# Attention in a fused hybrid network: test, mask load, division and norm in other places, and image 3's scores masked by VectorE

## The chip, the cores and the metric

The kernel runs on one NeuronCore of one Trainium2 chip. The metric is the time on the device in microseconds (us). The engines of a core run side by side, each through its own queue in order: PE (TensorE, matrix products, with PEld for its weight loads), DVE (VectorE), ACT (ScalarE), POOL (GpSimd) and SP (SyncE, which issues DMAs here).

## What is computed

The reference is a chain of six layers over four images of 32 x 32 positions and 256 channels (L = 1024 tokens per image). Layer 0 is a selective scan (Mamba-like) with 512 inner channels and 64 states; then come a grouped convolution, the attention with which this change deals, a mixture of 8 experts, a second selective scan with 16 states, and a second mixture. The attention, per image, with 8 heads of 32 channels:

```python
Q, K, V = (proj(Wq, bq), proj(Wk, bk), proj(Wv, bv))
scores = jnp.einsum('bhnd,bhmd->bhnm', Q, K) / jnp.sqrt(jnp.float32(hd))
mask = jnp.zeros((N, N), dtype=bool).at[edge_index[0], edge_index[1]].set(True)
scores = jnp.where(mask[None, None], scores, -jnp.inf)
attn = jax.nn.softmax(scores, axis=-1)
attended = jnp.einsum('bhnm,bhmd->bhnd', attn, V)
out = attended @ Wo + bo
y = x + out            # then a layer norm, times gamma, plus beta
```

The two scans are recurrences over the tokens, h = dA * h + (dt * x) * B and y = sum over states of h * C.

## The kernel before, in words

**Scans.** A scan is cut into units of 128 partitions (channels times states) by 1024 tokens, 1280 units in all. For a unit, SP loads dt broadcast into a tile dA, ACT takes its exp, PE spreads the input over the states into PSUM (`ps_rep`, two banks, tag x, two buffers), DVE multiplies `ps_rep` by B in place and runs the recurrence (`tensor_tensor_scan`), POOL multiplies by C, and after every second unit PE sums over the states (`ps_y`). `scans` (L351) writes this order: at step k it looks for chunks of input to load (`chunks_ahead`, L397), loads unit k+4, spreads unit k+1 (`first`), takes the exp of unit k+2 and scans unit k. The scans' order is `SCANS` (L31): layer 0 of image 0 and 1, layer 3 of image 0, and so on; layer 3 of image 3 is the last, and its input is made by image 3's stage "middle".

**Stages.** All else is written as Python generators in a list `STAGES` (L33): front (layer 0's projections), middle (`back0`, `layer1`, `attention`, `moe(2)`, `front3`) and last (`back3`, `moe(3)`), each for four images. `run` (L535) weaves them between the scans' instructions: after every half step of the scans it advances the current stage up to two yields, as long as a clock of planned costs per engine (`Metered`, whose `run` is the line L124 that nearly every instruction has) does not run ahead of DVE's. So the order on every engine's queue is fixed at build time. When a chunk's input has not been made within 5 units of its use (`LATEST`), `need` (L500) advances the stage until it has, with no scan units between. That happens once after the start: at unit 1211, five units before the last scan, image 3's stage "middle" is then run from inside attention through the mixture and into `front3`.

**PSUM.** The scans have five banks: `ps_rep` twice two banks, `ps_y` one. The stages have three, two of tag s and one of tag acc; `ps` (L173) hands these out in turn.

**Attention** (L1096). After a norm and a transpose, q, k and v are projected. `shift` (L1167) then tests whether scores can be large: it squares q and k on ACT, sums the squares by head with 64 matmuls of 4 columns (`ps_n2`), reduces on DVE, transposes, and makes a flag `large`. Each of PE, DVE, ACT and SP reads the flag and takes a branch (`tc.Switch`); the branch that finds row maxima is only for large scores and is not taken here, so `mT` stays at its memset's zero. Then the mask of 0 and -1e30 (bf16, 2 MB) is loaded by one DMA (L1149), and for each half nh of the queries and each pair of heads hp, `heads` (L1279) goes through 8 blocks of 128 keys: scores of two heads (`ps_sc`, the tag s, one bank each), plus `mT`, plus the mask through an identity matmul; exp on ACT into `p`; then the values and, through a matrix of ones, the sums, four matmuls side by side in 32 columns each (`ps_at`, tag acc). `pipe` (L179) sets values of block k-1 ahead of scores of block k. After two pairs DVE takes the reciprocal of the sums and POOL multiplies; after four, `attended` (L1325) projects by Wo (`ps_wo`), adds, norms (`lny`) and adds into tb.

Of the kernel before, what the change touches and what calls it, by code (L numbers as in the profile page):

```python
# [7 lines left out]
F32 = mybir.dt.float32  # L8
BF16 = mybir.dt.bfloat16
I32 = mybir.dt.int32  # L10
# [6 lines left out]
P = 128  # L17
# [115 lines left out]
class Hybrid:  # L133
# [217 lines left out]
    def scans(self, mp, psum):  # L351
# [16 lines left out]
        state = {}  # L368
        y = None
# [165 lines left out]
    def run(self):  # L535

        self.done, self.ready = set(), set()
        self.todo, self.stage, self.wait = list(STAGES), None, None
        nc, tc = self.nc, self.tc
# [532 lines left out]
    def prepare2(self, st, psum):  # L1072
# [5 lines left out]
        for k in range(2):  # L1078
# [8 lines left out]
        self.byhead = self.const.tile([P, 4], F32, name="byhead")  # L1087
        nc.vector.tensor_reduce(
            self.byhead, self.ident.rearrange("p (h d) -> p h d", d=HD), AX.X, ALU.add
        )  # L1090
        self.onesb = self.const.tile([P, P], BF16, name="onesb")
# [4 lines left out]
    def attention(self, b, tb):  # L1096
        nc, tc, vec = self.nc, self.tc, self.vec
        with tc.tile_pool(name=f"at{b}", bufs=1, side="right") as op:
# [4 lines left out]
            mT = op.tile([P, 2, L], BF16, name="mT")  # L1103
            wo = self.weight(op, "L2_attn_Wo", 2)
            with tc.tile_pool(name=f"aa{b}", bufs=1, side="right") as fp:
# [24 lines left out]

                def values(j):
# [13 lines left out]
            with tc.tile_pool(name=f"ab{b}", bufs=1, side="right") as fp:  # L1145
                yield from self.shift(fp, qT, kT, mT)
            with tc.tile_pool(name=f"ac{b}", bufs=1, side="right") as fp:
                maskT = fp.tile([P, TB, L], BF16, name="maskT")
                nc.sync.dma_start(maskT, self.mem[("maskT",)].rearrange("j p f -> p j f"))  # L1149
                yield 1.0  # L1150
                for nh in range(2):
                    raw, sums = (
                        fp.tile([P, 2, 512], F32, tag=t, name=t) for t in ("raw", "sums")
                    )
                    for hp in range(4):
                        yield from self.heads(fp, raw, sums, qT, kT, v, maskT, mT, nh, hp)
                        if hp % 2:
                            c = hp // 2
                            nc.vector.reciprocal(sums[:, c, :], sums[:, c, :])
                            yield 2.0  # L1160
                            nc.gpsimd.tensor_tensor(
                                raw[:, c, :], raw[:, c, :], sums[:, c, :], ALU.mult
                            )
                            yield 0.5
                    yield from self.attended(fp, tb, nh, raw, xa, wo)

    def shift(self, fp, qT, kT, mT):  # L1167
# [3 lines left out]
        nc, tc = self.nc, self.tc  # L1171
        nc.vector.memset(mT, 0.0)
        n2 = self.ps("ps_n2", (P, 2, TB * HEADS))
        for i, x in enumerate((qT, kT)):
            sq = fp.tile([P, 2, L], F32, tag="sq", name="sq")
            for c in range(2):
                nc.scalar.activation(sq[:, c, :], x[:, c, :], AF.Square)
                yield 0.5
                for m in range(TB):
                    at = 4 * (2 * m + c)  # L1180
                    nc.tensor.matmul(
                        n2[:, i, at : at + 4], lhsT=sq[:, c, m * P : (m + 1) * P], rhs=self.byhead,
                        start=True, stop=True,
                    )
                yield 1.5
        top = fp.tile([P, 2], F32, name="top2")
        nc.vector.tensor_reduce(top, n2, AX.X, ALU.max)
        yield 0.5
        ps = self.ps("ps_n3", (P, 2, P))
        for i in range(2):  # L1190
            nc.tensor.transpose(ps[:1, i, :], top[:, i : i + 1], self.ident)
        yield 0.5
# [6 lines left out]
        large = fp.tile([1, 1], I32, name="large")  # L1199
        nc.vector.tensor_copy(large, most[:, 0:1])  # L1200
        yield 1.0
        yield 1.0
# [6 lines left out]
        for arm in tc.Switch(go, 2):  # L1209
            if arm == 1:  # L1210
                for _ in self.row_max(fp, qT, kT, mT):
                    pass
# [3 lines left out]
    def row_max(self, fp, qT, kT, mT):  # L1216
# [3 lines left out]
        mask = fp.tile([P, TB, L], BF16, name="mask")  # L1220
        nc.sync.dma_start(mask, self.mem[("maskT",)].rearrange("j p f -> p j f"))
# [57 lines left out]
    def heads(self, fp, raw, sums, qT, kT, v, maskT, mT, nh, hp):  # L1279

        nc = self.nc
        qs = slice(nh * 512, (nh + 1) * 512)
        c, at = hp // 2, 64 * (hp % 2)
        acc = self.psum.tile([P, 512], F32, tag="acc", name="ps_at", bufs=1)
        got = {}

        def scores(kb):
            two = [self.psum.tile([P, 512], F32, tag="s", name="ps_sc", bufs=2) for _ in range(2)]  # L1290
# [6 lines left out]
            for i in range(2):  # L1297
                nc.tensor.matmul(
                    two[i], lhsT=self.onesb[rows[i], :], rhs=mT[rows[i], c, qs],
                    start=False, stop=False,  # L1300
                )
            for i in range(2):
# [3 lines left out]
            got[kb] = p = fp.tile([P, 2, 512], F32, tag="p", name="p", bufs=3)  # L1306
            for i in range(2):
                nc.scalar.activation(p[:, i, :], two[i], AF.Exp)

# [11 lines left out]
        yield from self.pipe(range(TB), scores, values, cost=1.3, cut=True)  # L1321
# [3 lines left out]
    def attended(self, fp, tb, nh, att, xa, wo):  # L1325
# [19 lines left out]
        yield from self.pipe(range(2), project, add, cost=1.7)  # L1345
        yield from self.norm(fp, y, 4, y, "lny")
# [443 lines left out]
```

## Time and profile before

| what | us |
|---|---|
| median of 3 runs (6886.66 to 6919.45) | 6898.74 |
| the profiled execution | 6903.87 |
| its span | 6902.1 |
| mT's memsets in the four attentions, at | 1474.0, 2609.0, 4064.1, 5520.6 |
| last scan before the stretch without scans, at | 5645.6 |
| last head's reciprocal of image 3, at | 5851.2 |

| group (128 partitions) | mean ns of one | count |
|---|---|---|
| DVE scan 1024 | 2285 | 1280 |
| DVE product with `ps_rep` 1024 | 1213 | 1280 |
| POOL product 1024 | 2371 | 1280 |
| ACT exp of scores 512 | 595 | 512 |
| DVE reciprocal 512 | 3353 | 16 |
| PE mask product `ps_sc` 512 | 397 | 512 |

A row of a profile's timeline has the start in us, the duration, the engine, the line, the operation, what it writes and reads, its size and how many rows are merged (xN); in brackets stands the idle time of the engine before it and what ended that. A row of the windows view has the stretch, its length, then the busy time of PE, PEld, DVE, ACT and POOL with their instructions, the granted clock of PE (1.00 is full), the share of the DMA engines and GB/s. Records of PE with f32 operands come twice per matmul.

### The profile page before, as it was taken

What the parts mean: (1) busy time and instruction counts of PE and PEld (TensorE: products, weight loads), DVE (VectorE), ACT (ScalarE), POOL (GpSimd) and SP (SyncE); (2) the same over time, 40 slices, a digit from 0 to 9 for tenths busy, and PEclk for the clock granted to TensorE, in tenths of its full rate; (3) what the DMA queues carried; (4) which work ended last, traced back from release to release, by engine and by line L of the source; (5) the groups of instructions that cost most, each with busy time, mean ns of one, the idle gap of its engine ahead of it and who ended that gap; (6) DMA issues with size and microseconds to landing.
All of it is one profiled execution on the core that took longest, in us unless ns stands there. A gap on an engine that the chain in (4) does not pass through costs nothing. (4 is left out here: it accounts for less than half of the span.)

```text
span 6902.1 us, 66302 instructions
## 1 busy us (share of the span) xinstructions
PE 5422.5 (79%) x20516; PEld 2221.7 (32%) x20516; DVE 5209.3 (75%) x4477; ACT 3437.1 (50%) x4143; POOL 3649.9 (53%) x1801
## 2 busy tenths in 40 slices
PE   6558768678798577879689768798798777867979
PEld 2002213232242032234145322252253322523556
DVE  7778988977898986889889867898899841247411
ACT  2426557344477343557568334477485432244411
POOL 0876776755557754555856545557666620044200
PEclk8558768679799577989789778898698789877989
DMA  1556665754455755446756654456667530145321
GB/s 71 149 143 162 175 176 154 188 136 111 113 164 158 195 145 132 116 127 177 185 151 163 173 136 119 122 144 177 179 165 185 149 86 6 44 122 155 86 61 34
DMA packets 394239, 937.47 MB, mean 136 GB/s; under 512 B 83220, under 2 KB 165729, under 8 KB 392225
## 3 DMA queue, kind: packets, MB, share of 16 engines
q1 hardware_dynamic: 391696, 930.53, 50.5%
q8 instruction: 173, 2.83, 0.2%
q0 software_dynamic: 2128, 2.13, 0.2%
q14 instruction: 242, 1.97, 0.1%
HBM read 842.59 MB, written 93.95 MB: 136 GB/s over the span
## 5 line engine op out<-in xcount | busy, mean ns | idle before, releaser
L124 POOL TENSOR_TENSOR h<-h,rows 128x1024 f32<-128x1024 f32 x1280 | 3030.9, 2371 | 1992.5 <-DVE h L124 1624.7
L124 DVE TENSOR_TENSOR_SCAN h<-dA,ps_rep 128x1024 f32<-128x1024 f32 x1280 | 2924.3, 2285 | 208.3 <-issue 91.3
L124 DVE TENSOR_TENSOR ps_rep<-ps_rep,rows 128x1024 f32<-128x1024 f32 x1280 | 1552.8, 1213 | 344.8 <-PE ps_rep L124 323.6
L124 ACT ACTIVATE dA<-dA,A_L_conv_A_log 128x1024 f32<-128x1024 f32 x1024 | 1152.4, 1145 | 712.4 <-DMA dA<-dt 623.2
L124 PE MATMUL ps_rep<-S,spread_L_conv_A_log 96*128 96x512 bf16 x2048 | 761.7, 463 | 739.7 <-DVE h L124 691.4
L124 PE MATMUL ps_y<-h,collect_L_conv_A_log 128*32 128x512 f32 x4096 | 780.4, 752 | 106.6 <-POOL h L124 105.6
L124 PE MATMUL ps_h<-xTm,we 128*128 128x512 f32 x1536 | 718.1, 607 | 4.3 <-ACT h_m L124 3.2
L124 PE MATMUL ps_e<-we,h_m 128*128 128x256 f32 x3072 | 702.1, 381 | 8.7 <-ACT h_m L124 8.7
L124 ACT ACT_TABLE_LOAD x486 | 623.5, 1283 | 73.8 <-PE ps_h L124 51.0
L124 PEld LDWEIGHTS <-spread_L_conv_A_log 96*128 96x128 bf16 x2048 | 163.6, 104 | 1502.1 <-DVE h L124 1167.0
L124 PEld LDWEIGHTS ps_e<-we,h_m 128*128 128x128 f32 x3072 | 580.5, 190 | 158.9 <-issue 54.0
L124 ACT ACTIVATE p<-ps_sc 128x512 f32<-128x512 f32 x512 | 277.9, 595 | 600.0 <-PE ps_sc L124 599.7
L124 DVE SCALAR_TENSOR_TENSOR tb<-ps_e,cw,tb 128x256 f32<-128x256 f32 x512 | 220.6, 474 | 407.4 <-PE ps_e L124 407.4
L124 ACT ACTIVATE h_m<-ps_h,cols 128x512 f32<-128x512 f32 x384 | 260.7, 687 | 487.5 <-PE ps_h L124 484.6
L124 ACT ACTIVATE dA<-dA,A_L_attn_A_log 128x1024 f32<-128x1024 f32 x256 | 293.5, 1148 | 407.8 <-DMA dA<-dt 376.2
L124 PE MATMUL ps_at<-p,v 128*32 128x512 f32 x1024 | 366.8, 631 | 64.2 <-ACT p L124 56.2
L124 PEld LDWEIGHTS ps_h<-xTm,we 128*128 128x128 f32 x1536 | 291.8, 193 | 339.7 <-issue 289.7
L124 PE MATMUL ps_rep<-S,spread_L_attn_A_log 96*128 96x512 bf16 x512 | 191.3, 464 | 225.4 <-DVE h L124 183.3
L124 PE MATMUL ps_sc<-qT,kT 32*128 32x512 f32 x1024 | 305.0, 671 | 0.0
L124 PE MATMUL ps_at<-p,ones 128*32 128x512 f32 x1024 | 282.2, 631 | 0.0
L124 PEld LDWEIGHTS ps_y<-h,collect_L_conv_A_log 128*32 128x32 f32 x4096 | 102.0, 119 | 493.1 <-POOL h L124 254.1
L124 PE MATMUL ps_cv<-pad,diag 128*128 128x512 f32 x576 | 260.4, 593 | 0.0
(304 smaller groups left out, 5030.5 us busy)
## 6 DMA issues: line engine op xcount, KB each, us to landing
dA<-dt SPq DMA_DIRECT2D x2048, 256.0 KB
dA<-dt SPq DMA_DIRECT2D x2048, 64.0 KB
we<-in_L_ffn_W_dram SPq DMA_DIRECT2D x64, 512.0 KB
parts<-parts SPq DMA_DIRECT2D x64, 384.0 KB
S<-parts SPq DMA_DIRECT2D x96, 256.0 KB
dt<-sp_r SPq DMA_DIRECT2D x64, 256.0 KB
y<-yo SPq DMA_DIRECT2D x128, 128.0 KB
y_back<-y SPq DMA_DIRECT2D x64, 256.0 KB
```

The costliest lines, as they stand in the source:

```text
L124: return got(*args, **kw)
```

## The change

1. The test leaves `shift` and becomes `large_scores`, called after the projections of q and k and ahead of the values. Its sums take 8 matmuls of 512 columns, four side by side, with a `byhead` repeated 8 times; the branch stays where it was.
2. `maskT` moves to attention's outer pool, and its load is issued right after the test.
3. Division, projection and norm of the first half are woven into later heads: after the third yield of a head, each yield is followed by one of a waiting generator `then`. A division goes into the head behind it, the projection of half 0 after the first head of half 1, and its norm into the second.
4. In `scans`, when a chunk's input is late, the next unit's `first` is put off, the unit is finished, and only then is `need` called, with a flag `alone`.
5. Heads that begin with `alone` set make the mask 0 or 1 once, keep their scores in the scans' PSUM (two banks as one tile, two buffers), take one exp over 1024 columns, and mask on DVE: min with 3e38, times the mask. Their pipe has three steps: scores, mask, values. Other heads are as before.

```diff
-        def chunks_ahead(k):
-
-            if k + AHEAD < len(units) and units[k + AHEAD][2:] == (0, 0, 0):
+        def chunks_ahead(k, late=False):
+            if not late and k + AHEAD < len(units) and units[k + AHEAD][2:] == (0, 0, 0):
                 waiting.append(k + AHEAD)
             while waiting:
                 scan, d = units[waiting[0]][:2]
-                if waiting[0] - k > LATEST and ("parts", *scan, d) not in self.ready:
-                    break
+                if ("parts", *scan, d) not in self.ready:
+                    if waiting[0] - k > LATEST:
+                        break
+                    if not late:
+                        return True
+                    self.alone = True
                 chunk(waiting.pop(0))
+                self.alone = False
+            return False
...
-            chunks_ahead(k)
+            waits = chunks_ahead(k)
             load(k + 4)
-            first(k + 1)
+            if not waits:
+                first(k + 1)
...
+            if waits:
+                chunks_ahead(k, True)
+                first(k + 1)
             yield
...
+    def all_heads(self, fp, tb, qT, kT, v, maskT, mT, xa, wo):
+        nc = self.nc
+        def divided(raw, sums, c):
+            nc.vector.reciprocal(sums[:, c, :], sums[:, c, :])
+            yield 2.0
+            nc.gpsimd.tensor_tensor(raw[:, c, :], raw[:, c, :], sums[:, c, :], ALU.mult)
+            yield 0.5
+        then = iter(())
+        self.zero_one = False
+        for nh in range(2):
+            raw, sums = (fp.tile([P, 2, 512], F32, tag=t, name=t, bufs=2) for t in ("raw", "sums"))
+            for hp in range(4):
+                for n, cost in enumerate(self.heads(fp, raw, sums, qT, kT, v, maskT, mT, nh, hp)):
+                    yield cost
+                    if n >= 3:
+                        more = next(then, None)
+                        if more is not None:
+                            yield more
+                yield from then
+                then = iter(())
+                if nh and hp == 0:
+                    y = yield from self.projected(fp, 0, first, xa, wo)
+                    then = self.normed(fp, tb, 0, y)
+                if hp % 2:
+                    then = divided(raw, sums, hp // 2)
+            first = raw
+        yield from then
+        y = yield from self.projected(fp, 1, raw, xa, wo)
+        yield from self.normed(fp, tb, 1, y)
...
+    def large_scores(self, fp, qT, kT, large):
...
+        for i, x in enumerate((qT, kT)):
             for c in range(2):
+                nc.scalar.activation(sq[:, i, c, :], x[:, c, :], AF.Square)
+                yield 0.8
+        for g in range(2):
+            n2 = self.ps("ps_n2")
+            for r in range(4):
+                nc.tensor.matmul(
+                    n2[32 * r : 32 * r + 32, :], lhsT=self.byhead.rearrange("p h k -> p (h k)"),
+                    rhs=sq[:, r // 2, r % 2, g * 512 : (g + 1) * 512],
+                    start=True, stop=True, tile_position=(0, 32 * r),
+                )
+            nc.vector.tensor_reduce(top[:, g : g + 1], n2, AX.X, ALU.max)
+            yield 1.3
...
+        alone = self.alone
+        if alone and not self.zero_one:
+            self.zero_one = True
+            for kb in range(TB):
+                nc.vector.tensor_scalar(maskT[:, kb, :], maskT[:, kb, :], -1.0, None, ALU.is_ge)
...
         def scores(kb):
-            two = [self.psum.tile([P, 512], F32, tag="s", name="ps_sc", bufs=2) for _ in range(2)]
+            if alone:
+                both = self.scan_psum.tile([P, 2, 512], F32, tag="x", name="ps_sx", bufs=2)
+                two = [both[:, i, :] for i in range(2)]
+            else:
+                two = [self.psum.tile([P, 512], F32, tag="s", name="ps_sc", bufs=2) for _ in range(2)]
...
+            if alone:
+                nc.scalar.activation(p, both, AF.Exp)
+                return
...
+        def masked(kb):
+            nc.vector.scalar_tensor_tensor(
+                got[kb], got[kb], 3.0e38, maskT[:, kb, qs].unsqueeze(1).to_broadcast([P, 2, 512]),
+                ALU.min, ALU.mult,
+            )
...
-        yield from self.pipe(range(TB), scores, values, cost=1.3, cut=True)
+        if alone:
+            yield from self.pipe(range(TB), scores, masked, values, cost=1.3)
+        else:
+            yield from self.pipe(range(TB), scores, values, cost=1.3, cut=True)
```

More of the change, by code (lines that the diff above doesn't have):

```diff
@@ L368, in scans @@
         state = {}
+        self.scan_psum = psum
         y = None
@@ L538, in run @@
         self.todo, self.stage, self.wait = list(STAGES), None, None
+        self.alone = False
         nc, tc = self.nc, self.tc
@@ L1086, in prepare2 @@
         nc.vector.tensor_scalar(self.bq, vec["L2_attn_bq"], self.isq, None, ALU.mult)
-        self.byhead = self.const.tile([P, 4], F32, name="byhead")
+        byhead = st.tile([P, 4], F32, name="byhead4")
         nc.vector.tensor_reduce(
-            self.byhead, self.ident.rearrange("p (h d) -> p h d", d=HD), AX.X, ALU.add
+            byhead, self.ident.rearrange("p (h d) -> p h d", d=HD), AX.X, ALU.add
         )
+        self.byhead = self.const.tile([P, 4, 8], F32, name="byhead")
+        nc.vector.tensor_copy(self.byhead, byhead.unsqueeze(2).to_broadcast([P, 4, 8]))
         self.onesb = self.const.tile([P, P], BF16, name="onesb")
@@ L1103, in attention @@
             mT = op.tile([P, 2, L], BF16, name="mT")
+            maskT = op.tile([P, TB, L], BF16, name="maskT")
             wo = self.weight(op, "L2_attn_Wo", 2)
+            large = op.tile([1, 1], I32, name="large")
+            nc.vector.memset(mT, 0.0)
             with tc.tile_pool(name=f"aa{b}", bufs=1, side="right") as fp:
@@ L1129, in attention @@
                 )
+                yield from self.large_scores(fp, qT, kT, large)
+                nc.sync.dma_start(maskT, self.mem[("maskT",)].rearrange("j p f -> p j f"))
                 def values(j):
@@ L1145, in attention @@
             with tc.tile_pool(name=f"ab{b}", bufs=1, side="right") as fp:
-                yield from self.shift(fp, qT, kT, mT)
+                yield from self.shift(fp, qT, kT, mT, maskT, large)
             with tc.tile_pool(name=f"ac{b}", bufs=1, side="right") as fp:
[L1148 to L1173, printed above, removed]
+                yield from self.all_heads(fp, tb, qT, kT, v, maskT, mT, xa, wo)
+    def all_heads(self, fp, tb, qT, kT, v, maskT, mT, xa, wo):
[27 more added lines that the diff above has]
+        yield from self.normed(fp, tb, 1, y)
@@ L1174, in shift @@
+    def large_scores(self, fp, qT, kT, large):
+        nc = self.nc
+        sq = fp.tile([P, 2, 2, L], F32, name="sq")
+        top = fp.tile([P, 2], F32, name="top2")
         for i, x in enumerate((qT, kT)):
-            sq = fp.tile([P, 2, L], F32, tag="sq", name="sq")
             for c in range(2):
[L1177 to L1192, printed above, removed]
+                nc.scalar.activation(sq[:, i, c, :], x[:, c, :], AF.Square)
[10 more added lines that the diff above has]
+            yield 1.3
@@ L1193, in shift @@
+        nc.vector.tensor_tensor(top[:, 0:1], top[:, 0:1], top[:, 1:2], ALU.max)
+        ps = self.ps("ps_n3", (P, 2, 64))
+        nc.tensor.transpose(ps[:1].rearrange("o i r -> o (i r)"), top[:, 0:1], self.ident)
         most = fp.tile([1, 2], F32, name="most")
@@ L1198, in shift @@
         nc.vector.tensor_scalar(most[:, 0:1], most[:, 0:1], -1.0, 1.0, ALU.mult, ALU.add)
-        large = fp.tile([1, 1], I32, name="large")
         nc.vector.tensor_copy(large, most[:, 0:1])
-        yield 1.0
-        yield 1.0
+        yield 0.5
+    def shift(self, fp, qT, kT, mT, maskT, large):
+        nc, tc = self.nc, self.tc
         E = mybir.EngineType
@@ L1210, in shift @@
             if arm == 1:
-                for _ in self.row_max(fp, qT, kT, mT):
+                for _ in self.row_max(fp, qT, kT, mT, maskT):
                     pass
@@ L1214, in shift, with row_max @@
         yield 1.0
-    def row_max(self, fp, qT, kT, mT):
+    def row_max(self, fp, qT, kT, mT, mask):
         nc = self.nc
-        mask = fp.tile([P, TB, L], BF16, name="mask")
-        nc.sync.dma_start(mask, self.mem[("maskT",)].rearrange("j p f -> p j f"))
         m3 = fp.tile([P, TB, HEADS, 32], BF16, name="m3")
@@ L1299, in scores @@
                     two[i], lhsT=self.onesb[rows[i], :], rhs=mT[rows[i], c, qs],
-                    start=False, stop=False,
+                    start=False, stop=alone,
                 )
+            got[kb] = p = fp.tile([P, 2, 512], F32, tag="p", name="p", bufs=3)
+            if alone:
+                nc.scalar.activation(p, both, AF.Exp)
+                return
             for i in range(2):
@@ L1305, in scores @@
                 )
-            got[kb] = p = fp.tile([P, 2, 512], F32, tag="p", name="p", bufs=3)
             for i in range(2):
                 nc.scalar.activation(p[:, i, :], two[i], AF.Exp)
+        def masked(kb):
[3 more added lines that the diff above has]
+            )
         def values(kb):
@@ L1319, in values, with projected @@
                 )
-        yield from self.pipe(range(TB), scores, values, cost=1.3, cut=True)
+        if alone:
+            yield from self.pipe(range(TB), scores, masked, values, cost=1.3)
+        else:
+            yield from self.pipe(range(TB), scores, values, cost=1.3, cut=True)
         nc.scalar.copy(raw[at : at + 64, c, :], acc[:64, :])
         nc.scalar.copy(sums[at : at + 64, c, :], acc[64:, :])
-    def attended(self, fp, tb, nh, att, xa, wo):
+    def projected(self, fp, nh, att, xa, wo):
         nc = self.nc
@@ L1345, in attended, with normed @@
         yield from self.pipe(range(2), project, add, cost=1.7)
+        return y
+    def normed(self, fp, tb, nh, y):
+        nc = self.nc
         yield from self.norm(fp, y, 4, y, "lny")
```

## The prediction

> **What bounds the kernel now.** I first read the page's slices. DVE carries the scans and is nearly full for 32 of 40 slices; then comes a hole, and near the end PE is full instead.
>
> ```profile
> PE   6558768678798577879689768798798777867979
> ...
> DVE  7778988977898986889889867898899841247411
> ...
> POOL 0876776755557754555856545557666620044200
> ```
>
> So there are three regimes: to about 5642 us DVE sets the pace (1211 of 1280 scan units, a product of 1.21 and a scan of 2.29 us each, 3.5 together); then image 3's middle stage runs with no scan beside it; then come the last scans and the last mixture-of-experts stage. The windows view of image 2's attention and of image 3's stretch:
>
> ```profile
> 4064.00:4102.00 38.00, 21.95 (x92) 15.29 (x94) 14.78 (x14) 11.15 (x11) 13.89 (x7) 0.54 0.42 97
> 4102.00:4190.00 88.00, 71.35 (x352) 18.73 (x352) 52.57 (x30) 34.20 (x51) 35.45 (x15) 0.84 0.52 135
> 4190.00:4285.00 95.00, 77.35 (x382) 22.52 (x378) 77.33 (x57) 45.70 (x66) 46.64 (x22) 0.87 0.44 114
> 4285.00:4450.00 165.00, 143.65 (x743) 40.69 (x742) 133.24 (x93) 80.14 (x116) 91.98 (x43) 0.92 0.44 115
> ...
> 5642.00:5704.00 62.00, 52.55 (x250) 12.60 (x250) 5.84 (x3) 19.89 (x37) 3.61 (x2) 1.00 0.04 10
> 5704.00:5738.00 34.00, 24.03 (x66) 8.54 (x68) 7.72 (x17) 7.04 (x14) 6.28 (x5) 0.65 0.00 0
> 5738.00:5851.00 113.00, 96.53 (x462) 22.81 (x458) 3.35 (x1) 35.95 (x66) 1.26 (x1) 1.00 0.00 1
> ```
>
> The third number after the length is DVE's busy time: in image 2's attention (4064 to 4450) it sums to 278 of 386 us, 108 idle; the same sums give 91 for image 0 (1474 to 1835) and 105 for image 1 (2609 to 2987). Elsewhere DVE is idle some 9% (90 of 993 us between two attentions), so attention is where the scans lose time. The waits view, of DVE and of PE (us in total, times, longest), names what moves:
>
> ```profile
> DVE sums L124 <- ACT sums L124: 226.7, 16, 69.9
> ```
>
> ```profile
> PE ps_sc L124 <- DMA maskT<-maskT: 39.3, 4, 12.1
> ```
>
> The first is DVE, in order, standing before the division until the head has ended (37 us of it in images 0 to 2); the second is PE standing before the first mask product. Last, the PE timeline of one key block with no scan beside it:
>
> ```profile
> 5648.26 1.13 PE L124 MATMUL ps_sc<-qT,kT 32*128 32x512 f32 x4
> 5649.22 0.38 PE L124 MATMUL ps_sc<-mT,onesb 32*128 32x512 bf16 x2
> 5649.54 0.60 PE L124 MATMUL ps_sc<-maskT,identb 128*128 128x512 bf16 x2
> 5650.67 1.11 PE L124 MATMUL ps_at<-p,v 128*32 128x512 f32 x3 [0.53 <-ACT p L124]
> ...
> 5652.15 1.13 PE L124 MATMUL ps_sc<-qT,kT 32*128 32x512 f32 x4
> ```
>
> A block takes 3.89 us and is a loop: scores, exp, values, and only then the next scores, because two PSUM banks hold just one block. Beside the scans it takes 4.0.
>
> **Part 1, images 0 to 2: test, mask load, division, norm.** DVE's work is nearly the same, so what is saved is its idle time. In image 1 the gaps before DVE instructions are: 12.1+3.6+1.1 around the test, 4.7 at the branch, 17.0+2.0 from the mask load, 12.7 before four divisions, some 14 at the two projections.
> - Test: 64 matmuls with 4 columns (four runs of 3.58, 14 us of PE) become 8 packed four across; four `ps_at` products of that shape take 0.97 to 1.5, so 2 to 3 us, plus two reductions of 512 (0.7 each, as the 128x512 rows from PSUM) in place of one of 0.29. Added wait: DVE stands before each reduction for PE, the queued scan products behind it, and PE's next spread behind those. I keep 6 of the 17 us. Squares stay (1.04 each).
> - Branch: stays. PE's jump took 5.42 us there, so I keep 5; only the wait for the flag itself goes, since it is made four projection steps earlier.
> - Mask load: one DMA, moved on SP past the values' steps; its issue is 0.39, the units' loads queued behind it shift by no more. It lands about 9 us after issue (issued 5563.7, PE released 5572.5), and now has four projection steps and 16 additions as cover. If that cover failed, the 9 to 12 us come back per image.
> - Division and norm of the first half go in among the next head's steps. DVE no longer stands before three of four divisions (10 us) and PE not before the first projection (4.8); 8 of the 14 us at the projections go. The last division and projection stay exposed.
>
> But a head itself keeps its loop: 8 blocks of 3.95 to 4.1, 32 to 33 us. In the order in which the changed program's instructions stand, 51 scan units lie between the starts of an image's first and last head where 56 lay; with the last head's own, about 58 and 64. That is 58 x 3.5 + 25 of other DVE work = 228 in 8 x 33.3 = 267 us, so 39 idle. With 6+5 for test and branch and 8 at the end, some 60 us of idle stay: saved 31, 45 and 48, sum 124. Counted on PE instead: image 1's heads took 315 us and would take 267, but 6 units (21 us) move out: 27, plus 11 of the test, so 38, 38 and 30, sum 106. I take 115; bounds 40 (the idle time only changes its name) and 165 (image 2's idle falls to the usual 9%).
>
> **Part 2, image 3 up to the stretch alone.** The same savings, test 11, mask 15, one division 4.5, less the slack of one more head (14) and one more unit (3.5): 13. In the new order three heads, not two and a bit, come before the last scan. Bounds 0 to 25. The stretch then starts at 5642-115-13 = 5514.
>
> **Part 3, the stretch alone.** Before, from 5642 to the end of the last head (5850.5, by the division at 5851.2) it is 208.5 us. After, five heads stand there. Per block:
> - removed: two mask products (0.48 of PE), and the second exp's start; one exp over 1024 takes 1.13 (two took 1.09; the 128x1024 exp from SBUF 1.15).
> - added: a DVE product of p and mask, 128x1024. Nearest row: SCALAR_TENSOR_TENSOR y_back 128x1024 from SBUF, 1.26 at the least, 1.28 median, 3.46 at the most. The Trainium skill ("SBUF — State Buffer", Who interferes with whom) speaks against this: a DVE instruction with two SBUF inputs contends with a GpSimd one that reads SBUF. That explains the 3.46 (a POOL product is 2.37), and by the rule each product would cost up to 3.6. But the rows above show POOL busy 3.6 of 62 us there. I take 1.27.
> - PE per block: scores and ones 1.28 (5648.26 to 5649.54), values 0.97 (beside scans, when both halves of p are there; 1.48 above has a wait for the second half in it): 2.25.
> - Loop: scores' end to values' start is 1.13+1.27 and about 0.45 of hand-overs (0.3 to ACT, 0.05 and 0.1 onward) = 2.85; then 2.25 of PE. Two blocks are in flight (two double banks), so 5.1/2 = 2.55 per block. The product waits for ACT; behind it on DVE stand only the next products and a few divisions, and PE's values wait for it. The scan's banks are free once the last unit's scan has read them.
>
> Filling and draining the three steps costs about 1.5 us twice per head, in place of nothing: 22.6 a head, I take 23.5 (31.1 before). Five heads 117. Around them: eight passes that make the mask 0 or 1, on DVE before the first product, waiting for the last old head; no row is near, the skill ("VectorE: DVE Perf Modes", The perf-mode tier table) gives 693 ns for 2048 bf16, so an estimate of 0.43 each, 3.4, at single rate 9.8; I take 4. The projection inside 5 (16 records took 5.8 at half clock). Two divisions (3.35) delay a product by 2 each; the first half's norm 4. Sum 134, saved 74; bounds 40 and 90. The 5.4 and 4.7 us holes of PE (5702 to 5722) go, and with them the half clock to 5738: the skill ("TensorE: Matmul & The Clock Gate", HAM oscillation) warns only of gaps over about 3.4 us. By that rule the bubbles of 1.5 us leave the clock full; the trace shows it full with a 0.53 hole per block. What is costlier than the rule says is the way back: the clock was not full again until 5738, 16 us after the last long hole.
>
> **Part 4, behind it.** The queued unit's spread is now made after the stage, so DVE waits for two matmuls (0.53) and a hand-over, 1 us; one unit fewer is left, 3.5 less. The mixture, image 3's front and the 790 us after keep their order. I set 0, bounds -4 to +2.
>
> **Sum.** 115+13+74 = 202. The profiled execution took 6903.9, the median of three is 6898.7, 5 lower. 6903.9-202 = 6702, less 5: 6697, rounded to 6700.
>
> **Rivals.**
> - *Only the stretch alone pays* (0.2). In images 0 to 2 a head is still a 4 us loop, and with fewer units per head DVE idles in other places. Part 1 gives 40: 6899-40-13-74 = 6772. For it: PE is busy 87% in 4285 to 4450 already. Against: gaps of 17 and 12 us have named causes.
> - *Only the attention windows pay* (0.13). The mask product takes over: a slower form or POOL beside it gives 2.5, so (2.85+1.23+2.25)/2 = 3.2 per block and 28 a head; 5 x 28+17 = 157, saved 51, and with more exposed at the division 30: 6899-128-30 = 6741.
> - *All idle goes* (0.1): 165+25+90 = 280: 6619.
> - *Slower* (0.03): the division and norm inside heads delay the scan products, PE stands for over 3.4 us in each head and falls to half clock, where a block took 6.08 instead of 3.89 (5721 to 5738). At 2.2 us a block it decides from 202/2.2 = 92 of the 192 blocks of images 0 to 2; with all of them it is 6899+420-202 = 7117. Against: with two divisions and a norm in it, 4285 to 4450 had a granted clock of 0.92.
> - The likeliest (0.54): its own range 6660 to 6740.
>
> That it does nothing can be excluded: the built order has 40 merged exps in image 3. Under 0.5% (34 us) a measurement of this kernel can't tell from no change. Range 6630 to 6780; faster 0.95, same 0.02, slower 0.03.
>
> **What would show it.** Mask products near 1.27 and 40 exps of 1.13; heads alone 23 to 24 us apart; DVE idle near 60 us per attention; no wait of PE for the mask; stretch alone starting near 5514 and its last head ending near 5650. Wrong if heads of images 0 to 2 are over 35 us, or PE's clock falls in them.

## The result, and the profile after

| kernel | median us | profiled execution, us | last scan before the stretch alone, at | last head's end, at |
|---|---|---|---|---|
| before | 6909.1 (4 runs) | 6903.9 | 5645.6 | 5849.9 |
| after | 6826.4 (4 runs) | 6823.6 | 5595.3 | 5769.8 |

The changed kernel takes 0.9888 of the time before (95% interval 0.9853 to 0.9922), so it is faster by 1.1%. The forecast was 6700, range 6630 to 6780: the sign is right, the size is not, 83 us by the medians in place of 202. Between the two profiled executions it is 80 us, which divide so: 28 us up to scan unit 1190 (5517.0 and 5488.9), which is the part of images 0 to 2; 22 from there to the last scan before the stretch; 30 in the stretch (204.3 and 174.5, from that scan to the last head's end); nothing behind it (1052.2 and 1052.1). Forecast were 115, 13, 74 and 0. The stretch now holds 42 blocks of keys where it held 46; at 3.89 us a block, that alone is some 16 of its 30 us.

The slices of the page after, to be held against those of before:

```profile
PE   6558778679797568979689679798797788967979
...
DVE  8778988978798997889889877898899863247411
```

DVE's row has hardly a digit more than before. The windows view of the changed kernel (length, then PE, PEld, DVE, ACT, POOL, PE's clock): the heads of images 0, 1 and 2, then image 3's heads alone, piece by piece.

```profile
1487.00:1767.20 280.20, 268.60 (x1389) 71.14 (x1390) 218.37 (x137) 142.98 (x210) 148.03 (x66) 0.97 0.45 116
2620.40:2903.70 283.30, 270.29 (x1399) 74.01 (x1400) 216.97 (x135) 145.25 (x213) 148.16 (x66) 0.99 0.48 123
4062.50:4348.40 285.90, 270.75 (x1399) 74.37 (x1400) 218.81 (x136) 145.02 (x213) 149.10 (x67) 0.99 0.47 121
...
5637.00:5672.00 35.00, 34.16 (x117) 7.13 (x113) 12.91 (x9) 9.34 (x10) 2.05 (x1) 0.51 0.00 1
5672.00:5676.00 4.00, 4.00 (x21) 3.19 (x20) 0.99 (x2) 1.16 (x2) 0.00 (x0) 1.00 0.00 0
5676.00:5699.00 23.00, 17.66 (x112) 4.26 (x108) 12.90 (x23) 10.59 (x13) 0.00 (x0) 1.00 0.00 1
5699.00:5735.00 36.00, 35.16 (x118) 7.40 (x116) 13.00 (x9) 10.92 (x14) 7.96 (x5) 0.50 0.00 0
5735.00:5770.00 35.00, 34.16 (x113) 7.00 (x112) 9.81 (x8) 9.27 (x11) 0.00 (x0) 0.50 0.00 0
```

The heads of images 0, 1 and 2 before:

```profile
1501.90:1813.20 311.30, 279.31 (x1420) 74.24 (x1422) 237.12 (x147) 147.85 (x215) 159.27 (x71) 0.92 0.45 120
2647.60:2960.70 313.10, 274.39 (x1424) 76.67 (x1424) 238.10 (x148) 148.85 (x218) 159.72 (x71) 0.92 0.48 125
4101.60:4420.10 318.50, 279.61 (x1424) 77.09 (x1424) 238.81 (x148) 148.97 (x218) 159.73 (x71) 0.90 0.47 123
```

They held 64 scan units each; now it is 58. Two things stand here. In the heads of images 0 to 2 PE is now busy 95 to 96% of the time (88 to 90% before), while DVE is idle for 62, 66 and 67 us (length less busy time). And of the heads alone, one takes 23 us with the clock at 1.00; the others take 34 to 36, most of it or all at half clock, with PE busy 98%. The PE timeline shows what the clock does to one block of keys:

```profile
5608.98 2.08 PE L124 MATMUL ps_sx<-qT,kT 32*128 32x512 f32 x4
...
5613.28 2.08 PE L124 MATMUL ps_sx<-qT,kT 32*128 32x512 f32 x4
...
5680.40 1.13 PE L124 MATMUL ps_sx<-qT,kT 32*128 32x512 f32 x4
...
5682.66 1.13 PE L124 MATMUL ps_sx<-qT,kT 32*128 32x512 f32 x4
```

A block takes 4.30 us at half clock and 2.26 to 2.45 at full clock, where 2.55 was forecast. The waits view of DVE and of PE, for the two lines shown of before:

```profile
DVE sums L124 <- ACT sums L124: 15.7, 4, 4.6
```

```profile
PE ps_sc L124 <- ACTq L1249: 34.7, 3, 12.8
```

The wait before the division fell from 226.7 to 15.7 us and the wait of PE for the mask is gone; at the first scores PE now stands for the branch (this line has three of the four images). In all four images PE stood 69 us for branch and mask before (29.5 and 39.3), and stands 41 now. So the waits that the change was aimed at did go, and yet little time came of it. Of the division's 226.7, only 37 had stood in images 0 to 2, beside the scans.

### The profile page after: what moved, and what is told of

Read it like the earlier page. It is cut to its first block, busy times and chain, and to the rows that moved or that the text cites. A ratio compares the mean times of both kernels' runs of the same rounds, so it can differ in the third digit from the quotient of the medians.

```text
span 6821.9 us, 65779 instructions
## 1 busy us (share of the span) xinstructions
PE 5400.3 (79%) x20240; PEld 2170.9 (32%) x20240; DVE 5275.1 (77%) x4534; ACT 3446.8 (51%) x4112; POOL 3653.0 (54%) x1801
## 5 line engine op out<-in xcount | busy, mean ns | idle before, releaser
L124 PE MATMUL ps_y<-h,collect_L_conv_A_log 128*32 128x512 f32 x4096 | 795.5, 757 | 96.4 <-POOL h L124 94.9
L124 ACT ACTIVATE p<-ps_sc 128x512 f32<-128x512 f32 x432 | 234.4, 594 | 448.8 <-PE ps_sc L124 436.7
L124 PE MATMUL ps_at<-p,v 128*32 128x512 f32 x1024 | 382.1, 666 | 52.5 <-ACT p L124 31.9
L124 PE MATMUL ps_at<-p,ones 128*32 128x512 f32 x1024 | 299.6, 667 | 0.0
L124 PE MATMUL ps_sc<-qT,kT 32*128 32x512 f32 x864 | 251.1, 653 | 41.3 <-ACTq L1249 34.7
```

The costliest lines, as they stand in the source:

```text
L124: return got(*args, **kw)
```

## The experiments

All ratios are to the kernel before on the same chip, five rounds each (four without the ones' product). What is said to be over or under the changed kernel is a difference of medians from different sessions: the kernel before had medians of 6897 to 6909 in them, and the changed kernel's own ratio is known to 0.0034 only, some 24 us. "By the ratios" below is the difference of two ratios times the 6900 us of before. A difference of less than some 25 us from the changed kernel is not clear by the times, and the profiles have to show it. Theory A said that two other bounds stepped in: PE's own work in the heads of images 0 to 2, and half clock in the heads alone. The rivals are named with each run.

**1. Which half of the change pays: the order alone.** Image 3's heads stay as they were, in two banks and with PE's mask.

```
-        alone = self.alone
+        alone = False
```

> The changed kernel with image 3's heads as in the kernel before (two banks, mask product on PE, two exps); the moved test, mask load, division and norm stay. Theory A (the gain of images 0 to 2 and of image 3 up to the stretch is what the changed trace shows, 47 us, and the stretch alone pays 33 us at half clock): the stretch takes about 200 instead of 176 us, time about 6850, 23 to 33 us over the changed kernel. Rival B (the heads in the scans' PSUM have an effect outside the stretch too, or none of the gain comes from the order): within 10 us of the changed kernel, or near 6900. TensorE's clock: A expects 1.0 in the heads alone, as in the kernel before.

Measured: 6817.2, ratio 0.9866 (0.9845 to 0.9887), no slower than the changed kernel. The stretch from the last scan to the last head's end took 167.1 us at full clock, against 174.5. A's full clock came, but its "stretch of about 200" was wrong, since the order alone takes 37 us out of the stretch (204.3 to 167.1): some 16 because it holds 42 blocks instead of 46, the rest because the moved norm and division take the holes with them, and the 23.9 us of half clock that stood there before. That part of the 74 us belongs to the order. So the scores in the scans' PSUM with the mask on DVE bring nothing measurable as they stand; B had that number, but not its reason, for outside the stretch the two profiles differ by no more than 19 us at any unit, and the order does gain.

**2. Is it the clock, and what does the clock go by?** Two products more per block, read by nobody, with the full array or a quarter of its rows; and four such products once per head where PE stands anyway, with the division cut in pieces.

```
             if alone:
                 nc.scalar.activation(p, both, AF.Exp)
+                for i in range(2):
+                    w = self.psum.tile([P, 512], F32, tag="s", name="ps_warm", bufs=2)
+                    nc.tensor.matmul(w, lhsT=self.identb, rhs=maskT[:, kb, qs], start=True, stop=True)
                 return
```

In the narrow run lhsT and rhs are cut to `[:32]`; in the fill run the loop is `if kb == 1: for i in range(4)`, and `divided` takes four reciprocals of 128 columns when alone.

> The changed kernel with two more products in each key block of the heads alone, 128 rows x 128 columns x 512, bf16, into a bank that nobody reads: PE's work of the removed mask products, without anything that waits for it. Theory A (the half clock in the heads alone comes of how little of the array is in use per time, not of idle time): with 0.6 us MORE of PE work per block the clock is full in most of the stretch, a block takes 2.85 to 3.0 instead of 4.30, a head 26 to 28 instead of 30, time 10 to 20 us under the changed kernel. Rival B (the half clock comes of the idle stretches before the first values of a head and behind the division, and stays by itself): the clock stays half, a block takes 4.30 + 0.6 x 2 = 5.4 and time is about 35 us over the changed kernel.

> As the run before it, but the two extra products have 32 rows (a quarter of the array) and the same 512 columns, so the same time on PE. Theory A (share of the array in use): the clock stays half in the heads alone, a block takes 5.4, time 25 to 40 us over the changed kernel. Rival B2 (the clock goes by the number of products or by PE's busy time, whatever their shape): the same as with the full products.

> The changed kernel with four full-array products only once per head alone, behind the second block's scores, where PE stands 1.45 us for the first mask product, and with the division of a head alone cut into four pieces of 128 columns between the mask products, so that the 3.63 us hole of PE goes. Theory A2 (full clock is lost only in a 3.4 us window with little in use, at the head's start and at the division, and once lost the heads' own work doesn't bring it back): the clock stays full through all five heads, blocks of 2.36, heads of 24, the stretch about 176 - 4 x 6.3 = 151, time about 25 us under the changed kernel. Rival (the steady blocks themselves are too little, so the clock falls anyway): half clock from the second or third block of each head, time within 8 us of the changed kernel.

Measured: full 6790.2 (0.9835, 0.9820 to 0.9850), narrow 6799.6 (0.9860, 0.9836 to 0.9885), fill 6769.9 (0.9812, 0.9794 to 0.9829). More work on PE made the kernel faster by 36 us, so the stretch waited for PE's clock and not for the amount of its work. All three gain more than A had (36, 27 and 56 us), since I had set a head at half clock to 30 us and a full one to 24, where 34.7 and 21.2 were measured; and the narrow products were to slow the kernel by A. The table has each head alone, from the start of its scores to the next head's (the second has the 3.7 us projection in it), and the time at half clock in the stretch:

| kernel | heads alone, us | at half clock | stretch |
|---|---|---|---|
| after | 34.0, 38.4, 24.0, 35.1, 35.1 | 135.8 | 174.5 |
| two full products per block | 23.5, 27.7, 26.8, 30.0, 23.5 | 17.1 | 139.5 |
| two narrow ones | 21.2, 27.5, 27.7, 40.7, 23.0 | 54.6 | 148.0 |
| four full ones per head | 21.2, 24.8, 23.5, 23.9, 21.2 | 6.8 | 122.6 |
| mask kept on PE (run 5) | 22.7, 26.4, 22.7, 30.0, 22.8 | 10.2 | 132.4 |
| norm behind the heads (run 3) | 21.2, 24.8, 21.1, 21.1, 21.2 | 0 | 117.4 |

The fill run answers for the cause: the steady blocks are the same as in the changed kernel, and they hold full clock by themselves; so they do in runs 3 and 6, which have the same four products. The clock is lost in a short stretch with little work, at a head's start and behind a hole of 3.63 us. This is the head's start, in the changed kernel:

```profile
5604.42 1.02 PE L124 MATMUL ps_sx<-qT,kT 32*128 32x512 f32 x4
5605.28 0.38 PE L124 MATMUL ps_sx<-mT,onesb 32*128 32x512 bf16 x2
5607.11 1.07 PE L124 MATMUL ps_at<-p,v 128*32 128x512 f32 x2 [1.45 <-DVE p L124]
...
5608.98 2.08 PE L124 MATMUL ps_sx<-qT,kT 32*128 32x512 f32 x4
```

PE stands 1.45 us for the first mask product, and the trace's clock record turns to half at 5606.7. Once the clock is lost, a head's own blocks don't bring it back: the half clock lasted 64.8 and 81.9 us in the changed kernel. The windows view of the narrow run, then of the full one, each for the head in which the clock was lost:

```profile
5684.50:5725.00 40.50, 40.50 (x132) 9.73 (x128) 14.47 (x9) 9.63 (x11) 5.66 (x5) 0.50 0.00 0
```

```profile
5684.00:5714.00 30.00, 29.16 (x130) 6.39 (x132) 13.70 (x9) 9.43 (x11) 6.24 (x5) 0.76 0.00 1
```

With narrow products PE was busy every moment of 40 us and stayed at half clock; with full ones it was back after 17 us. That speaks for a gate that goes by how much of the array is in use and not by busy time alone.

The clock records hold a second sign of it. In the six traces whose heads alone are as light as the changed kernel's (its own and the five of run 4), the half clock ended 15 times, always at a head's end or in the projection behind it: the last 3.41 us before it held only values (four products side by side that fill all 128 rows) or the projection (128 x 128), at most with a head's last or first records of the narrow products (32 rows) at the edge. It never ended among the blocks, which are scores and values by turns. Against it stand: one episode each for the full and the narrow run; two short spells of the narrow run (6.8 and 3.4 us), which ended among blocks; and that the bubble at the first head's start cost the clock in four of the six traces only. With the test put back (below) the first head alone kept full clock, in 21.3 us, through the same bubble. So the rule of the gate is supported, not settled.

**3. The hole that is left.** The norm of the first half stands in a head. Of the changed kernel's timeline:

```profile
5693.40 0.16 DVE L124 TENSOR_SCALAR lny_v<-lny_mv 128x4 f32<-128x4 f32 x1
...
5694.52 1.28 ACT L252 ACT_TABLE_LOAD   x1
5695.81 0.20 ACT L124 ACTIVATE lny_r<-lny_v 128x4 f32<-128x4 f32 x1
...
5696.28 0.16 DVE L124 TENSOR_TENSOR lny_w<-lny_r 128x4 f32<-128x4 f32 x1 [2.72 <-ACT lny_r L124]
...
5696.97 1.22 DVE L124 SCALAR_TENSOR_TENSOR p<-p,maskT 128x1024 f32<-128x1024 f32 x1
...
5698.24 0.62 PE L124 MATMUL ps_at<-p,v 128*32 128x512 f32 x2 [3.63 <-DVE p L124]
```

The root needs a table that ACT must load behind an exp; DVE waits for the root; the mask product is queued behind that wait, and PE's values behind the product. The run adds to the fill run (and gives `y_at` a second buffer):

```
-                    then = self.normed(fp, tb, 0, y)
+                    held = None
+                    if self.alone:
+                        held = y
+                    else:
+                        then = self.normed(fp, tb, 0, y)
...
+        if held is not None:
+            yield from self.normed(fp, tb, 0, held)
```

> The kernel with four full-array products per head alone and divided reciprocals, and also with the first half's norm, when the heads are alone, put behind the last head instead of into a head. In the run before, a 3.63 us hole of PE was left in one head: the norm's root makes ACT load a table (1.28 us), DVE waits 2.72 us for the root, and the mask product stands behind it. Theory A: that hole and the half clock behind it (6.8 us) go; the norm at the end is hidden in part by the wait for the last division: 3 to 8 us under the run before, so near 6764, and a full clock from the first to the last head alone. Rival: the norm costs at the end what it saves (0 to +4).

Measured: 6761.5 (0.9805, 0.9792 to 0.9819), no half clock in the stretch, four heads of 21.1 or 21.2 us, a stretch of 117.4 instead of 122.6. The profile is as theory A expected; by the times alone the two runs can't be told apart.

**4. What the order's parts are worth, and what sets the pace beside the scans.** First the two halves of the reordering put back, one at a time (in the first, `large_scores`, the mask's load and `row_max`'s own copy of it stand at the branch again; in the second, `all_heads` calls `divided`, `projected` and `normed` behind their heads).

> The changed kernel with the test (in its new, packed form) and the mask's load back at the branch, where they were in the kernel before. Theory A (these two waits are worth what DVE's idle time between the large flag and the first head shows: 12.8, 23.2 and 18.0 us before, 8 to 9 after, of which the test's own reductions keep some 3.4): 15 to 30 us over the changed kernel in all four images. Rival B (PE sets the pace in attention, so what is idle there is made good in the heads): within 8 us of it. PE's wait for the mask is back: 9 to 12 us per image, as before.

> The changed kernel with the divisions, the first half's projection and both norms back behind their heads; test and mask load stay moved, the heads alone stay in the scans' PSUM. Theory A: DVE's waits for the division (37 us before, 12 after in images 0 to 2) and for the projections come back, and in image 3's stretch alone PE has holes of about 5 us behind each second head: 25 to 50 us over the changed kernel. Rival B (PE sets the pace in images 0 to 2, and at half clock in the stretch the holes were hidden anyway): under 12 us.

Measured: test and load back 6868.4 (0.9961, 0.9948 to 0.9975), 42 us over the changed kernel (50 by the ratios) and more than either theory had; up to unit 1190 it loses 30 us, in image 3 before the stretch 19 more. Division and norms back: 6842.6 (0.9923, 0.9909 to 0.9936), 16 us over by the medians, 24 by the ratios and 31 between the profiled executions, which leaves open whether it reaches A's 25: up to unit 1190 the profile loses 11 us, and in the stretch 25, where PE stands again for 4.9, 7.2 and 3.5 us and the heads alone went by at half clock for 173 us, 199.6 us in place of 174.5. So the test and the load are the larger part of the gain, the smaller in my sum of named gaps.

Then PE's load in the heads: the product of ones with mT is left out beside the scans.

```
-            for i in range(2):
+            for i in range(2 if alone else 0):
                 nc.tensor.matmul(
                     two[i], lhsT=self.onesb[rows[i], :], rhs=mT[rows[i], c, qs],
```

> The changed kernel without the product of the ones with the row maxima mT in the heads that are not alone (it leaves out the subtraction of the row maxima there; mT is zero in this execution): 0.32 us of PE less in each of 64 blocks of images 0 to 2 and 24 of image 3, 69 us of PE in all; no instruction of DVE, ACT, POOL or a queue changes. Theory A (in the heads of images 0 to 2 it is PE, 92% busy, that sets the pace, and so DVE's idle time of 58 to 68 us per image's heads stays): heads of 33 instead of 35.5 us, DVE idle in the heads down by 12 to 20 us per image, time 35 to 65 us under the changed kernel. Rival B (the wait for DVE and the order set it, PE has slack): less than 12 us.

Measured: 6825.8 (0.9895, 0.9878 to 0.9912), nothing gained. By the expectation that is rival B. But the heads did get shorter, 280, 283 and 286 to 267.5, 272.5 and 273.5 us, and the windows hold 53 scan units instead of 58: the planner charges its clock of PE for every product, saw cheaper heads, and moved 5 units out of each image's heads. My "no instruction of DVE changes" was wrong. So the run was made again with the charge kept, which keeps the order:

```
+                if not alone:
+                    self.clock["tensor"] += matmul_us(two[i], self.onesb[rows[i], :])
+                    continue
                 nc.tensor.matmul(
```

> The same as the run without the ones' product (it leaves out the subtraction of the row maxima in the heads that are not alone; mT is zero in this execution), but the planner's clock of PE is still charged for it, so that the order of the work stays that of the changed kernel: 58 scan units in each image's heads, not 53. In the run before, the planner saw cheaper heads and took 5 units out of each image's heads, 17.5 us of DVE work, which ate the gain. Theory A (PE sets the pace in the heads): the heads of an image take 262 to 268 instead of 280 to 286 us, DVE's idle time in them falls from 58 to 64 to some 42 to 48, time 40 to 60 us under the changed kernel. Rival B (PE has slack): under 12 us.

Measured: 6778.6 (0.9814, 0.9797 to 0.9831), 48 us under the changed kernel. The windows of the heads of images 0 to 2:

```profile
1485.80:1752.80 267.00, 250.92 (x1239) 64.66 (x1262) 218.17 (x137) 143.08 (x210) 147.93 (x66) 0.97 0.45 122
2603.60:2878.50 274.90, 255.46 (x1249) 68.63 (x1272) 216.63 (x135) 144.96 (x213) 147.39 (x66) 0.97 0.47 126
4033.00:4309.50 276.50, 254.48 (x1249) 68.29 (x1272) 217.64 (x136) 145.08 (x213) 148.09 (x66) 0.98 0.47 125
```

DVE's busy time is that of the changed kernel; PE has 15 to 18 us less to do, and the heads are 8 to 13 us shorter, DVE's idle time by the same. So PE sets the larger part of the pace there, not all of it: heads of 262 to 268 us, as A had them, came in image 0 alone. Up to unit 1190 the profile gains 42 us; its stretch then lost 13 at half clock.

Last the other way round: PE's work stays, and more scan units are put beside it.

```
         def scores(kb):
+            if self.image_at < 3:
+                self.clock["tensor"] += 0.6
```

Here `image_at` is the number of the image, which `attention` now notes.

> The changed kernel with nothing but the planner's clock changed: in the heads of images 0 to 2 it is charged 0.6 us more of PE per key block, which sets 70 instead of 58 scan units beside an image's heads. The 12 units come out of stretches in which the next stage waited for a scan (50, 15 and 15 units of waiting, 35, 1 and 1 left), so image 3's attention still starts at the same unit. Theory A (the planner's clock has 228 us of PE in an image's heads where PE is busy 270, so PE sets the pace and DVE idles): heads take 295 to 310 us with 70 units, DVE idle in them falls from 58 to 64 to 25 to 40, time 50 to 90 us under the changed kernel. Rival B (the idle time comes with each unit, by the hand-over from PE to DVE, 1.0 to 1.1 us per unit): idle grows to 70 to 75 per image, time within 15 us of the changed kernel or over it.

Measured: 6692.7 (0.9693, 0.9671 to 0.9716), 134 us under the changed kernel, more than A expected. The profiled executions differ by 124, of which 120 are there by unit 1190 and nothing comes in the stretch (174.0). The same windows, now with 72 to 73 units:

```profile
1493.30:1784.90 291.60, 276.62 (x1460) 73.30 (x1484) 266.18 (x167) 157.96 (x224) 181.39 (x81) 0.97 0.52 139
2573.40:2876.00 302.60, 279.48 (x1459) 74.18 (x1484) 262.79 (x164) 160.78 (x228) 179.12 (x80) 0.96 0.52 140
3977.40:4284.10 306.70, 280.44 (x1459) 74.61 (x1484) 263.60 (x165) 160.21 (x228) 179.19 (x81) 0.96 0.51 138
```

For 14 to 15 units more, which are some 50 us of DVE, PE is busy only 8 to 10 us more and the heads are only 11 to 21 us longer; DVE idles 25, 40 and 43 us instead of 62, 66 and 67. DVE's wait for the spread product, over the whole run, changed kernel first:

```profile
DVE ps_rep L124 <- PE ps_rep L124: 288.0, 197, 9.4
```

```profile
DVE ps_rep L124 <- PE ps_rep L124: 168.2, 99, 9.7
```

**5. The mask kept on PE, in the scans' double banks.** One half of the change in the heads alone without the other: one exp of 1024, `masked` left empty, the two identity products back.

> The changed kernel with one half of its change in the heads alone: scores in the scans' two double banks and one exp of 1024, but the mask stays a product of PE (128 x 128 x 512, bf16, twice per block), and VectorE multiplies nothing. PE's work per block is then 2.25 + 0.6 = 2.85 us. Theory A (what the heads alone lost was the clock, and the mask product on PE is enough work to keep or regain it): full clock but for some 20 us behind the norm's hole, a block takes 2.85 to 3.0, a head 25 to 27 instead of 34.7 at half clock, time 25 to 40 us under the changed kernel, so 6787 to 6801. Rival B (the scans' banks or the longer pipeline cause the half clock): half clock, blocks of about 5.4, over the changed kernel by 30 us or more.

Measured: 6775.4 (0.9824, 0.9810 to 0.9837), 51 us under the changed kernel. At full clock a head takes 31.1 us in two banks (run 1), 22.7 in the double banks with PE's mask and 21.2 with DVE's, and here all but 10.2 us of the stretch was at full clock. So the double banks, with their one exp and longer pipe, are what makes a head fast; moving the mask is worth 1.5 us per head at full clock and costs more than that as soon as the clock is lost. Theory A had the clock right, and a head (25 to 27) too long.

**6. All that helped together**: the norm-behind kernel with the charge of 0.6.

> All that helped together: four full-array products per head alone, the division of a head alone cut in four, the first half's norm behind the heads when alone, and 0.6 us more of PE per key block in the planner's clock in images 0 to 2. Theory A: the gains add, 50 to 90 us under the run with the norm at the end (6761.5), so 6670 to 6710. Rival B: within 15 us of 6761.5.

Measured: 6642.1 (0.9625, 0.9610 to 0.9640), 119 us under the kernel with the norm behind the heads, and 184 under the changed one: the gains add, and by more than A had, because the charge alone gave 134 instead of 50 to 90.

## Why the prediction was wrong, point by point

- **Part 1 (115 forecast, 28 measured up to unit 1190).** The failed step is "a head itself keeps its loop: 8 blocks of 3.95 to 4.1, 32 to 33 us", with 267 us for an image's heads. Measured were 280, 283 and 286. The period of 4.0 is what the loop takes with few units beside it; 58 units bring their own products, and PE does those too. The windows of before would have said so: PE was busy 280 us in image 2's heads, at a clock of 0.90. Six units fewer take off about 6 us (after, 270.8 less 64 blocks of 3.36 of PE, which is 215, leaves 0.96 per unit, the projection in it), so some 274 us was to be expected of PE. It was 269 to 271, so 267 left PE not even its busy time; on top of that PE stood for 12 to 15 us. DVE idle in the heads was set at 39 us per image; it was 62, 66 and 67, which is 78 of the 87 us missed. "Counted on PE instead" took only the difference of two heads' lengths, and so never met that sum.
- **Test, branch, mask load.** Right in kind: DVE idles 3.4 us at the test's reductions and 6.6 to 7.6 at the branch, where 6 and 5 were kept; PE's wait for the mask is gone. Run 4 prices test and load at 42 us in all four images (50 by the ratios).
- **Division and norm.** The waits went as forecast (226.7 to 15.7 in the view), at 16 us by run 4's medians and 24 by its ratios, which is not clear of the noise. Not forecast was that the norm's root holds up ACT's exps and, through DVE, PE, by 3.63 us.
- **Part 2 (13 forecast, 22 measured).** Right in sign; the last scan now comes with three heads before it, as the order said. The stretch began at 5595 instead of 5514 for part 1's sake.
- **Part 3 (74 forecast, 30 measured).** The durations held: mask product 1.22 (1.27 forecast), merged exp 1.02 (1.13), a block at full clock 2.35 (2.55). Of the eight passes over the mask seven took 0.40 to 0.41 (0.43); one took 2.60 beside a product of POOL (below), which made them 4.9 (4). In the sum for a head, eight blocks of 2.55 and twice 1.5 are 23.4, not the 22.6 written; 23.5 was used, so nothing hangs on it. The failed step is "by that rule the bubbles of 1.5 us leave the clock full". The bubble at the first head's start was followed by half clock, and four of five heads took 34 to 35 us plus the projection. With the clock all but held the stretch is 122.6 (run 2's fill) and 117.4 (run 3): 52 to 57 us lie in the half clock and in the holes that those runs closed, and with them closed the stretch would have saved 82 to 87. The Trainium skill ("TensorE: Matmul & The Clock Gate", What's actually happening) has full clock come back after one busy window of about 3.4 us; here PE was busy 98% of 36 us and more at 0.50. The measurement decides. I had the half clock as a rival, but in the heads of images 0 to 2, where the mask products stayed and the clock was 0.97 to 0.99.
- **Part 4 (0 forecast).** 0.1 us measured.
- **The rivals.** "Only the stretch alone pays" had part 1 right (40 against 28) and its reason, PE's 87% busy; it got 0.2. The half clock came on top, and no case of mine combined the two, so none came out at 6826. The slow mask product of "Only the attention windows pay" did not come (1.22).

What stays open: what the gate counts exactly, whether a bubble's place on the grid of 3.41 us (below) decides if it costs the clock, what beside PE holds the heads of images 0 to 2 (some four tenths of PE's relief did not come off them in images 1 and 2), and how much of the 42 us of test and load is the one and how much the other, which was not tried apart.

## What to carry to other kernels

Before a wait is priced as a gain, add up the busy time of the engine that would be next in the same window: at a given clock no stage gets shorter than that, and what it takes is more: here the sum of 269 to 271 us became 280 to 286. In a kernel whose order is planned by costs, look at what the planner does with a step that became cheaper: a clock of PE that was 0.6 us per block too cheap cost more (134 us) than the whole change won (83 us). When full-array products are taken off PE, look at the clock of what is left, at heads' starts and holes above all; a few products without a use, put where PE stands anyway, can be the cheapest repair.

## What the runs showed of the hardware that was not expected

- The granted clock changed only on a grid of 3.41 us: in the changed kernel's stretch it was half for 64.8 us, full for 27.3 and half for 81.9, which are 19, 8 and 24 times 3.41. A spell of half clock without full-array products in the blocks lasted 65 and 82 us in the changed kernel, with PE busy nearly all the time; with them it lasted 17 and 10 us.
- Loading ACT's table between exp and root (1.28 us) stopped PE for 3.63 us through two queues.
- A product of 128x1024 on DVE with a bf16 operand repeated over two heads took 1.22 us.
- Where DVE and POOL met, the later one took longer. In the trace of before, nine of the sixteen DVE products `y_back` took 1.26 to 1.28 us and seven 2.29 to 3.46; in each of the seven, and in none of the nine, a product of POOL was already running when it began, and DVE's ended 1.08 or 1.09 us after a POOL product had. Where POOL began 0.2 to 0.3 us after DVE, it was POOL's product that took 3.2 us instead of 2.37. It is the same with the passes that make the mask 0 or 1: the one of 2.60 us (5597.87 to 5600.47) began 0.09 us after a product of POOL (5597.78 to 5600.18); without the ones' product the passes stand apart, seven of them behind the end of that POOL product, and all eight took 0.40 to 0.43.
